# A kernel with a planned instruction order: shorter least time per scan unit in the plan, 1/std spread for two chunks at once, step sizes written to SBUF by VectorE

## The chip, the cores and the metric

The kernel runs on one core of one Trainium2 chip. The metric is the device time of one execution in microseconds (us). Before the change it is 8340.93 us, the median of three runs (8316.7 to 8378.94).

Five engines matter: TensorE (PE in the profile, its weight loads PEld), VectorE (DVE), ScalarE (ACT), GpSimd (POOL) and SyncE (SP, which here only issues DMAs). Each takes its own instructions strictly in program order and waits on semaphores for the others. SBUF is the working memory, PSUM (8 banks of 128x512 float32) is where TensorE writes.

## The reference

Four layers work on four images x of 96 channels and 64x64 pixels (L = 4096 positions). Cut to what matters:

```python
x = x + L0(_gn(x))        # layer norm, in-projection, 3x3 depthwise conv, silu,
                          # selective scan in 4 directions, layer norm, gate, out-projection
x = x + L1(_gn(x))        # deformable 3x3 conv: offsets and mask from a conv, 4 bilinear corners
t = t + L2_attn(_ln_t(t)) # FFT over the 4096 tokens, diagonal complex product, inverse FFT
t = t + L2_ffn(_ln_t(t))  # 96 -> 384 -> 96, fp8-like rounding
t = t + L3_attn(_ln_t(t)) # attention without softmax
t = t + L3_ffn(_ln_t(t))

# the selective scan, per image, direction k (4), channel d (192), state n (16):
delta = softplus(dts + delta_bias)            # the "step size"
h = exp(delta * A) * h + (delta * u) * B      # along 4096 positions
y = sum_n h * C
```

## The kernel before, in words

**Stages.** Layer 0 has a preparation per image (group norm, layer norm, convolution, `projected`, and `steps`, which makes the step sizes delta and delta*u) and the scan itself. `Layer0.behind` normalizes, gates and projects the scan's sum; `Layer1` computes offsets and then samples (`sample`: 1152 indirect gathers on GpSimd); `Fourier`, `Ffn`, `LinearAttention` and `Ffn` follow. Everything passes between the stages through DRAM, except for the last image.

**The scan is the metronome.** It is cut into 1536 units (4 images x 4 directions x 4 pieces of 1024 positions x 24 groups of 8 channels), one after the other. A unit has: a broadcast load of delta (L999, issued by ACT, 512 KB), exp on ACT (L1027), two bf16 matmuls that spread delta*u into a PSUM tile `db` (L1033), a product with B on VectorE (`enter`, L1047), the scan instruction on VectorE (`recur`, L1055), a product with C on GpSimd (`weigh`, L1064) and matmuls that sum over the state (`total`, L1078 and L1083).

**Everything else is woven in by a planner.** Two generator streams run beside the scan: `ends` (preparation of images 0 to 3, then layers 2 and 3 of every image) and `middle` (`behind` and layer 1 of every image). While the program is built, `Clock` keeps an estimated end for each engine. After each unit, `unit()` moves the plan's time `due` forward by `PACE` (L203, 4.5), and the plan's "now" is the later of `due` and the planned end of VectorE's queue (L224). Streams then add steps as long as each engine that a step uses is planned to be done no later than now plus a margin (`AHEAD`, L197). The costs given at each `yield cost(...)` are the planner's own. They set only the order: after building, every engine's instructions are tied to that order (`in_program_order`). When the last unit is placed, what is left of the streams follows by itself, with the scan's PSUM banks given to `ends` (`own_banks`: 5 banks for `ends`, 3 for `middle`; until then both share 3). I call this part the tail.

**PSUM banks in the plan.** A chain of steps may begin a step that needs a fresh bank only if `has_bank` allows (L289); `holds` says how many banks it keeps.

**Spread of 1/std.** Both layer norms (`normed_rows` L732 to L743, `normed` L1732 to L1745) keep 1/std of 8 chunks of 512 positions as rows of one 128x512 tile. `spread` (L527 to L532) brings one row to all partitions by a float32 matmul over all 128 rows with a column of the identity as weights (L531); VectorE then multiplies the chunk by it from PSUM (L738, L1742). One chain per chunk, three chains side by side.

**Step sizes.** `steps` (L827 to L900) runs 192 times, for one direction's 128 channels or two directions' 64. VectorE forms max(pd,0)+lw in place in PSUM (L856), multiplies it by u, still from PSUM, into `ex` (L861, L862, L868 or L874), and ACT copies it from PSUM to the SBUF tile `rl` (L877). SP stores `rl` to DRAM (L881). The bank is held until the copy is issued.

Of the kernel before, what the change touches and what calls it, by code (L numbers as in the profile page):

```python
# [14 lines left out]
AF = mybir.ActivationFunctionType  # L15
ALU = mybir.AluOpType
# [3 lines left out]
B, C, H, W = 4, 96, 64, 64  # L20
# [5 lines left out]
CH = 512  # L26
NCH = L // CH
# [155 lines left out]
def cost(pe=0.0, dve=0.0, act=0.0, pool=0.0, **more):  # L183
    return Step((pe, dve, act, pool), **more)


def wait(us=0.0, **more):

    return Step((0.0,) * 4, us, **more)
# [10 lines left out]

MARGIN = 0.5

PACE = 4.5  # L203


class Clock:
# [19 lines left out]
    def unit(self, scanned):  # L226

        self.due += PACE
        self.idle, self.beside = max(scanned, self.due), 0.0
# [42 lines left out]
def pipe(net, chains, width, every=0, lane=None, **tiles):  # L272


    chains, active = iter(chains), []
    clock, known, more = net.clock, net.known, True
    end, free = clock.now(), tiles
    while True:
        if more and len(active) < width:
            steps = next(chains, None)  # L280
            if steps is None:
                more = False
            else:
                active.append(Chain(steps, clock.now()))
                continue
        if not active:
            break
        for n, chain in enumerate(active):
            if chain.new and not net.has_bank(1 + (n > 0 and not active[0].holds)):  # L289
                continue  # L290
            if any(
                a.done <= chain.done + every
                for a in active[:n]
                if lane is None or (a.kind is lane) == (chain.kind is lane)
            ):
                continue
            if not all(free.get(tag, net.arrived.get(tag, 0)) > 0 for tag in chain.takes):
                continue
            if clock.has_room(known.get((chain.kind, chain.done), (1.0,) * 4), chain.ready):
                break  # L300
        else:
            yield BLOCKED
            continue
        for tag in chain.takes:
            if tag in free:
                free[tag] -= 1
        clock.precede(known.get((chain.kind, chain.done), (0.0,) * 4))
        step = next(chain.steps, None)
        if step is None:
            net.hold(-chain.holds)  # L310
            active.remove(chain)
            end = max(end, chain.ready)
            continue
        for tag in step.frees:
            free[tag] += 1
        known[chain.kind, chain.done] = step.work
        chain.ready = clock.queue(step, chain.ready)
        chain.done += 1
        net.hold(step.holds - chain.holds)
        chain.holds, chain.new, chain.takes = step.holds, step.new, step.takes  # L320
        yield None
    yield wait(max(0.0, end - clock.now()))
# [38 lines left out]
class Net:  # L361
# [165 lines left out]
    def spread(self, rstd, j, n, key):  # L527

        pb = self.mm(f"lnb{key}_{j}")
        row = self.ident[:, j : j + 1].to_broadcast([128, 128])  # L530
        self.nc.tensor.matmul(pb, lhsT=row, rhs=rstd, start=True, stop=True)  # L531
        return pb[:n]  # L532


# [24 lines left out]
class Layer0:  # L559
# [117 lines left out]
    @staticmethod  # L677
    def rows(pad, j):
        return pad[:, 1 + j * NR : 1 + (j + 1) * NR, 1 : 1 + W]

    @staticmethod
    def as_rows(t):
        return t.rearrange("p (h w) -> p h w", w=W)
# [25 lines left out]
    def normed_rows(self, b, x, pad):  # L709

        net, rows, as_rows = self.net, self.rows, self.as_rows
        tc, nc = net.tc, net.nc
        with tc.tile_pool(name=f"l0n{b}", bufs=2) as sm:
            for edge in (pad[:, 0, :], pad[:, PW - 1, :], pad[:, :, 0], pad[:, :, PW - 1]):
                nc.gpsimd.memset(edge, 0.0)
            yield wait(4.0)
            stats = []
            yield from net.group_norm_stats(x, sm, f"0_{b}", stats)
            mean, rstd = stats

            cen = sm.tile([C, 128], F32, name=f"cen{b}", tag="cen", bufs=1)
            nc.vector.tensor_scalar_mul(cen, net.cen96, rstd)
            yield cost(dve=0.3)
            net.hold(1)
            pb = net.mm(f"cb{b}")
            nc.tensor.matmul(pb[:, 0:1], lhsT=cen, rhs=mean, start=True, stop=True)
            bias = sm.tile([C, 1], F32, name=f"cenb{b}", tag="cenb", bufs=1)
            nc.scalar.mul(bias, pb[:C, 0:1], -1.0)
            net.hold(-1)
            yield cost(pe=0.3, act=0.3)  # L730

            rs = yield from net.centred(x, cen, lambda j: (rows(pad, j), as_rows), f"0_{b}", sm, bias)  # L732

            def chain(j):
                pb = net.spread(rs, 32 * (j % 4) + j // 4, C, f"0_{b}")
                yield cost(pe=1.2, holds=1)
                r = rows(pad, j)
                nc.vector.tensor_mul(r, r, as_rows(pb))  # L738
                yield cost(dve=0.7)
                nc.scalar.activation(r, r, AF.Identity, scale=net.vec(V_ING, C), bias=net.vec(V_INB, C))  # L740
                yield cost(act=0.8)

            yield from pipe(self.net, (chain(j) for j in range(NCH)), 3)  # L743

    def conv_weights(self, b, sm):

# [80 lines left out]
    def steps(self, b, ks, j, us, dtw, sm, xdbl):  # L827

        net = self.net
        nc = net.nc  # L830
        cs = slice(j * CH, (j + 1) * CH)
        tk = f"{b}_{j}_" + "".join(str(k) for k in ks)
        both = len(ks) == 2

        def tile_of(name, bufs):
            return sm.tile([128, CH], F32, name=f"{name}{tk}", tag=name, bufs=bufs)
# [4 lines left out]
        pd = net.mm(f"pd{tk}")  # L841
# [3 lines left out]
        ex = tile_of("ex", 3)  # L845
        nc.scalar.activation(ex, pd, AF.Abs)
        nc.scalar.activation(ex, ex, AF.Exp, scale=-1.0)
        lw, w1 = tile_of("lw", 2), tile_of("w1", 2)
        nc.scalar.activation(lw, ex, AF.Ln, bias=net.one)
        nc.scalar.activation(w1, ex, AF.Identity, bias=net.one)  # L850
        yield cost(pe=2.2 if both else 1.1, act=2.7, holds=1, takes="rl")
        nc.vector.scalar_tensor_tensor(w1, w1, -1.0, ex, ALU.add, ALU.subtract)  # L852
        yield cost(dve=0.7, holds=1)
        nc.gpsimd.tensor_sub(lw, lw, w1)  # L854
        yield cost(pool=1.3, holds=1)
        nc.vector.scalar_tensor_tensor(pd, pd, 0.0, lw, ALU.max, ALU.add)  # L856
        if both and ks[0] % 2 == ks[1] % 2:
            q, xc = ks[0] % 2, us[2]
            own, far = slice(64 * q, 64 * q + 64), slice(64 - 64 * q, 128 - 64 * q)
            turned = xc.rearrange("p (a b) -> p b a", a=64)  # L860
            nc.vector.tensor_mul(ex[own], pd[own], xc[own, cs])  # L861
            nc.vector.tensor_mul(  # L862
                ex[far].rearrange("p (a b) -> p a b", b=64),
                pd[far].rearrange("p (a b) -> p a b", b=64),
                turned[far, j * NR : (j + 1) * NR, :],
            )
        elif not both and ks[0] % 2:
            nc.vector.tensor_mul(  # L868
                ex.rearrange("p (w h) -> p w h", h=H),
                pd.rearrange("p (w h) -> p w h", h=H),  # L870
                us[1][:, j * NR : (j + 1) * NR, :],
            )
        else:
            nc.vector.tensor_mul(ex, pd, us[2 if both else 0][:, cs])  # L874
        yield cost(dve=1.4, holds=1, frees="lw")
        rl = tile_of("rl", 2)
        nc.scalar.copy(rl, pd)  # L877
        yield cost(act=0.6)
        parts = ((0, 64, ks[0], 128), (64, 128, ks[1], 128)) if both else ((0, 128, ks[0], 0),)
        for p0, p1, k, c0 in parts:  # L880
            nc.sync.dma_start(self.de_d[b][k][c0 : c0 + p1 - p0, cs], rl[p0:p1])  # L881
        yield wait(takes="du", frees="rl")

        du = sm.tile([128, 3, CH], BF16, name=f"du{tk}", tag="du", bufs=2)
        nc.scalar.copy(du[:, 0, :], ex)
# [7 lines left out]
            pr, lhsT=self.minus, rhs=du[:, 1, :], start=False, stop=True, skip_group_check=True  # L893
# [838 lines left out]
def normed(net, t, tl, key, pool, groups=(0, 1), arriving=False):  # L1732

    rs = yield from net.centred(
        t, net.cen96, lambda j: (tl[:C, j * CH : (j + 1) * CH], plain), key, pool, groups=groups, arriving=arriving
    )

    def chain(j):
        cs = slice(j * CH, (j + 1) * CH)
        pb = net.spread(rs, 32 * (j % 4) + groups.index(j // 4), C, key)  # L1740
        yield cost(pe=1.2, holds=1)
        net.nc.vector.tensor_mul(tl[:C, cs], tl[:C, cs], pb)  # L1742
        yield cost(dve=0.7)

    yield from pipe(net, (chain(j) for j in chunks(groups)), 3)  # L1745


def chunks(groups):
    return [4 * r + q for r in groups for q in range(4)]
# [324 lines left out]
```

## Time and profile before

| | us |
|---|---|
| median of three runs (lowest, highest) | 8340.93 (8316.7, 8378.94) |
| the profiled execution's own time | 8389.31 |
| its span, first to last instruction | 8387.5 |
| scan units, first scan to last scan's end | 191.6 to 7376.2 |
| tail after the last scan | 7376.2 to 8387.5 |
| sampling of the last image, all in the tail | 7497.7 to 7986.8 |
| layers 2 and 3 of image 2, end | 7910.5 |

The profile gives for every engine the busy time, for every group of equal instructions the count, mean duration and the idle time ahead of it with the releaser (what ended that wait), and for a stretch of time the busy time of each engine and the granted TensorE clock (1.0 is full speed). The mean granted clock of the execution is 0.790. A busy TensorE is not TensorE at its peak, since matmuls are pipelined and their ends modelled.

### The profile page before, as it was taken

To read this page: it belongs to the slowest core of one execution; us is meant where nothing else is said; L and a number is where in the kernel's file an instruction comes from. 1 tells how busy PE (TensorE), PEld (TensorE's weight loads), DVE (VectorE), ACT (ScalarE), POOL (GpSimd) and SP (SyncE) were. 2 spreads that over 40 slices of the span, in tenths; PEclk is the share of its full clock that TensorE was granted. 3 is DMA by queue.
4 is the path that set the end of the run, shared out by engine and by line. 5 is a ranking of instruction groups with operands and counts; after the bars stand their busy time and mean duration, and the time that the engine had idled before them with its cause. 6 is when DMAs were issued, how large, how long until landed. Compare 5 with 4: busy or idle time off the path is not lost.

```text
span 8387.5 us, 96574 instructions
## 1 busy us (share of the span) xinstructions
PE 6457.2 (77%) x32232; PEld 2791.3 (33%) x32232; DVE 6737.2 (80%) x5149; ACT 5007.3 (60%) x9177; POOL 5539.7 (66%) x4268
## 2 busy tenths in 40 slices
PE   6776777779767778877767888776888787887787
PEld 2211221122222233311222555221455332455473
DVE  2799889987799988777898888998887988846724
ACT  5665567646577877855667666644467766333324
POOL 0466556665578888656688888766688897626700
PEclk8876786778667878966677898786788887887798
DMA  3577678886778998876789899877799888844420
GB/s 91 160 213 201 170 191 223 224 196 185 190 213 242 248 250 220 216 184 176 216 221 243 220 233 235 189 174 181 192 229 243 209 217 207 181 107 130 133 67 13
DMA packets 791030, 1600.42 MB, mean 191 GB/s; under 512 B 285889, under 2 KB 374493, under 8 KB 788422
## 3 DMA queue, kind: packets, MB, share of 16 engines
q10 hardware_dynamic: 244224, 843.17, 39.3%
q1 hardware_dynamic: 472582, 524.50, 24.0%
q0 software_dynamic: 73728, 226.57, 10.2%
q8 instruction: 259, 4.24, 0.2%
q14 instruction: 237, 1.94, 0.1%
HBM read 1340.71 MB, written 253.14 MB: 190 GB/s over the span
## 4 chain that ended last, share of the span: by engine, by line
PE 31%; DVE 27%; DMA 11%; POOL 11%; ACT 9%; issue 8%; SPq 2%; ACTq 1%; DVEq 0%; another core or an unknown queue 0%; POOLq 0%
DVE da L1055 13%; POOL da L1064 7%; DVE db L1047 6%; PE pc L767 4%; PE f L1635 3%; PE py L1083 3%; PE ps L1528 3%; ACT g L1507 2%; POOL g L1495 2%; DMA da<-de 2%; ACT da L1027 2%; PE db L1033 2%; PE pd L1547 2%; DMA du<-du 2%; DMA m<-in_dft 1%
## 5 line engine op out<-in xcount | busy, mean ns | idle before, releaser
L1064 POOL TENSOR_TENSOR da<-da,bc 128x1024 f32<-128x1024 f32 x1536 | 3634.9, 2369 | 317.2 <-DVE da L1055 191.5
L1055 DVE TENSOR_TENSOR_SCAN da<-da,st,db 128x1024 f32<-128x1024 f32 x1152 | 2700.9, 2345 | 116.1 <-ACT da L1027 7.7
L1047 DVE TENSOR_TENSOR db<-db,bc 128x1024 f32<-128x1024 f32 x1536 | 1865.6, 1215 | 659.9 <-PE db L1033 644.2
L1027 ACT ACTIVATE da<-da,w_al 128x1024 f32<-128x1024 f32 x1536 | 1740.5, 1146 | 313.6 <-DMA da<-de 123.4
L1495 POOL DMA_INDIRECT g<-table,idx x1152 | 1191.1, 1034 | 408.1 <-issue 183.1
L1033 PE MATMUL db<-du,rep 24*128 24x512 bf16 x3072 | 687.4, 455 | 797.3 <-DVE da L1055 741.5
L1083 PE MATMUL py<-da,w_fold 128*32 128x512 f32 x6144 | 1103.2, 787 | 26.5 <-POOL da L1064 11.0
L1507 ACT ACTIVATE g<-g,wt 128x96 f32<-128x96 f32 x3456 | 966.0, 364 | 115.2 <-issue 19.0
L1055 DVE TENSOR_TENSOR_SCAN da<-da,db 128x1024 f32<-128x1024 f32 x384 | 877.2, 2284 | 66.1 <-ACT da L1027 31.7
L1528 PE MATMUL ps<-w_ident,g 128*96 128x128 f32 x3744 | 689.4, 331 | 224.5 <-ACT g L1507 67.3
L1033 PEld LDWEIGHTS <-rep 24*128 24x128 bf16 x3072 | 147.3, 93 | 1867.8 <-DVE da L1055 1128.9
L1528 PEld LDWEIGHTS ps<-w_ident,g 128*96 128x96 f32 x3744 | 500.0, 148 | 560.4 <-ACT g L1507 171.3
L1062 POOL COPY st<-da 128x1 f32<-128x1 f32 x1152 | 224.8, 195 | 697.7 <-DVE da L1055 664.4
L854 POOL TENSOR_TENSOR lw<-lw,w 128x512 f32<-128x512 f32 x192 | 244.3, 1272 | 660.7 <-DVE w L852 595.9
L767 PE MATMUL pc<-pad,wc 96*128 96x512 f32 x1152 | 570.6, 633 | 13.3 <-ACT xa L777 6.1
L1536 ACT COPY st<-ps 96x384 f32<-96x384 f32 x384 | 179.7, 472 | 483.1 <-PE ps L1528 418.8
L888 PE MATMUL pr<-ex,w_ident 128*128 128x512 f32 x384 | 297.3, 866 | 60.2 <-ACT st L1536 15.1
L767 PEld LDWEIGHTS pc<-pad,wc 96*128 96x128 f32 x1152 | 218.4, 200 | 313.9 <-issue 285.4
L844 PE MATMUL pd<-xd,w_dtw 103*64 103x512 f32 (+1 forms) x512 | 273.3, 798 | 57.3 <-ACT rl L877 15.2
L1547 PE MATMUL pd<-st,wdc 96*128 96x256 f32 x1152 | 303.8, 411 | 7.1 <-ACT st L1536 3.4
L1644 ACT COPY d<-f 128x512 f32<-128x512 f32 x192 | 111.6, 582 | 328.0 <-PE f L1635 274.1
L890 ACT CAST du<-pr 128x512 bf16<-128x512 f32 x192 | 111.7, 582 | 321.4 <-PE pr L889 259.7
(286 smaller groups left out, 8861.6 us busy)
## 6 DMA issues: line engine op xcount, KB each, us to landing
da<-de ACTq DMA_DIRECT2D x1536, 512.0 KB
du<-du SPq DMA_DIRECT2D x1536, 96.0 KB
bc<-bcd SPq DMA_DIRECT2D x128, 512.0 KB
y<-yb SPq DMA_DIRECT2D x384, 128.0 KB
de<-rl SPq DMA_DIRECT2D x128, 256.0 KB
m<-in_dft SPq DMA_DIRECT2D x128, 256.0 KB
ad<-y ACTq DMA_DIRECT2D x192, 128.0 KB
table<-pix SPq DMA_DIRECT2D x128, 192.0 KB
```

Source lines behind the costliest of these rows:

```text
L767: nc.tensor.matmul(pp, lhsT=wc[:, q, g * 128 : (g + 1) * 128], rhs=pad[:, r0 + dy : r0 + dy + NR, dx : dx + W], start=(q == 0), stop=(q == 8),
L888: nc.tensor.matmul(pr, lhsT=net.ident, rhs=ex, start=True, stop=False)
L1027: self.net.nc.scalar.activation(u.da, u.da, AF.Exp, scale=self.al[:, a : a + 1])
L1033: self.net.nc.tensor.matmul(db[:, h, :], lhsT=self.rep[64 * u.q + 32 * h : 64 * u.q + 32 * h + 24], rhs=u.du[64 * u.q + 32 * h : 64 * u.q ...
L1047: self.net.nc.vector.tensor_mul(u.db, u.db, u.bc[:, 0, :])
L1055: nc.vector.tensor_tensor_scan(u.along(u.hh), u.along(u.da), u.along(u.db), first, ALU.mult, ALU.add)
L1064: self.net.nc.gpsimd.tensor_mul(u.hh, u.hh, u.bc[:, 1, :])
L1083: nc.tensor.matmul(py[p0 : p0 + 32], lhsT=self.fold[:, u.i, :], rhs=hc[:, h * CH : (h + 1) * CH], start=u.sums["add"] is None and u.i == 0 ...
L1495: nc.gpsimd.indirect_dma_start(out=g[:, k, :], out_offset=None, in_=self.tables[b % 2], in_offset=bass.IndirectOffsetOnAxis(ap=idx[:, n : ...
L1507: nc.scalar.activation(pixel, pixel, AF.Identity, scale=wt[:, n, c : c + 1])
L1528: nc.tensor.matmul(pt[:, k, :], lhsT=g[:, k, c * C : (c + 1) * C], rhs=net.ident, is_transpose=True, start=(c == 0), stop=(c == corners - 1),)
L1547: nc.tensor.matmul(po, lhsT=wdc[:, k, :], rhs=st[k // 3][:, k % 3, :], start=(k == 0), stop=(k == 8))
```

## The change

Three edits. `PACE` goes from 4.5 to 4.3. The layer norms take two chunks per chain: both spreads are issued one after the other, each over only the 32 rows that hold its value, into two PSUM banks; a chain starts only when two banks are free, and two chains run side by side. In `steps`, VectorE writes the step size to the SBUF tile `rl` instead of PSUM, the product with u reads `rl`, ACT's copy is gone, and the planned hold of the bank ends with that write.

```diff
-PACE = 4.5
+PACE = 4.3
...
-            if chain.new and not net.has_bank(1 + (n > 0 and not active[0].holds)):
+            if chain.new and not net.has_bank(chain.new + (n > 0 and not active[0].holds)):
...
     def spread(self, rstd, j, n, key):
         pb = self.mm(f"lnb{key}_{j}")
-        row = self.ident[:, j : j + 1].to_broadcast([128, 128])
-        self.nc.tensor.matmul(pb, lhsT=row, rhs=rstd, start=True, stop=True)
+        k = slice(j - j % 32, j - j % 32 + 32)
+        row = self.ident[k, j : j + 1].to_broadcast([32, 128])
+        self.nc.tensor.matmul(pb, lhsT=row, rhs=rstd[k], start=True, stop=True)
         return pb[:n]
...
-    def chain(j):
-        cs = slice(j * CH, (j + 1) * CH)
-        pb = net.spread(rs, 32 * (j % 4) + groups.index(j // 4), C, key)
-        yield cost(pe=1.2, holds=1)
-        net.nc.vector.tensor_mul(tl[:C, cs], tl[:C, cs], pb)
-        yield cost(dve=0.7)
-
-    yield from pipe(net, (chain(j) for j in chunks(groups)), 3)
+    def chain(js):
+        yield wait(new=2)
+        pbs = [net.spread(rs, 32 * (j % 4) + groups.index(j // 4), C, key) for j in js]
+        yield cost(pe=1.2, holds=2)
+        for n, j in enumerate(js):
+            cs = slice(j * CH, (j + 1) * CH)
+            net.nc.vector.tensor_mul(tl[:C, cs], tl[:C, cs], pbs[n])
+            yield cost(dve=0.7, holds=1 - n)
+
+    js = chunks(groups)
+    yield from pipe(net, (chain(js[n : n + 2]) for n in range(0, len(js), 2)), 2)
```

`normed_rows` is changed in the same way. In `steps`:

```diff
         yield cost(pe=2.2 if both else 1.1, act=2.7, holds=1, takes="rl")
+        rl = tile_of("rl", 2)
...
-        nc.vector.scalar_tensor_tensor(pd, pd, 0.0, lw, ALU.max, ALU.add)
+        nc.vector.scalar_tensor_tensor(rl, pd, 0.0, lw, ALU.max, ALU.add)
+        yield cost(dve=0.7, frees="lw")
...
-            nc.vector.tensor_mul(ex, pd, us[2 if both else 0][:, cs])
-        yield cost(dve=1.4, holds=1, frees="lw")
-        rl = tile_of("rl", 2)
-        nc.scalar.copy(rl, pd)
-        yield cost(act=0.6)
+            nc.vector.tensor_mul(ex, rl, us[2 if both else 0][:, cs])
         parts = ((0, 64, ks[0], 128), (64, 128, ks[1], 128)) if both else ((0, 128, ks[0], 0),)
         for p0, p1, k, c0 in parts:
             nc.sync.dma_start(self.de_d[b][k][c0 : c0 + p1 - p0, cs], rl[p0:p1])
-        yield wait(takes="du", frees="rl")
+        yield cost(dve=0.7, takes="du", frees="rl")
```

The other two forms of the product (L861 and L862, L868) read `rl` in the same way.

More of the change, by code (lines that the diff above doesn't have):

```diff
@@ L734, in chain @@
             def chain(j):
-                pb = net.spread(rs, 32 * (j % 4) + j // 4, C, f"0_{b}")
-                yield cost(pe=1.2, holds=1)
-                r = rows(pad, j)
-                nc.vector.tensor_mul(r, r, as_rows(pb))
-                yield cost(dve=0.7)
-                nc.scalar.activation(r, r, AF.Identity, scale=net.vec(V_ING, C), bias=net.vec(V_INB, C))
-                yield cost(act=0.8)
-            yield from pipe(self.net, (chain(j) for j in range(NCH)), 3)
+                yield wait(new=2)
+                pbs = [net.spread(rs, 32 * ((j + i) % 4) + (j + i) // 4, C, f"0_{b}") for i in range(2)]
+                yield cost(pe=1.2, holds=2)
+                for i in range(2):
+                    r = rows(pad, j + i)
+                    nc.vector.tensor_mul(r, r, as_rows(pbs[i]))
+                    yield cost(dve=0.7, holds=1 - i)
+                    nc.scalar.activation(r, r, AF.Identity, scale=net.vec(V_ING, C), bias=net.vec(V_INB, C))
+                    yield cost(act=0.8, holds=1 - i)
+            yield from pipe(self.net, (chain(j) for j in range(0, NCH, 2)), 2)
     def conv_weights(self, b, sm):
@@ L860, in steps @@
             turned = xc.rearrange("p (a b) -> p b a", a=64)
-            nc.vector.tensor_mul(ex[own], pd[own], xc[own, cs])
+            nc.vector.tensor_mul(ex[own], rl[own], xc[own, cs])
             nc.vector.tensor_mul(
                 ex[far].rearrange("p (a b) -> p a b", b=64),
-                pd[far].rearrange("p (a b) -> p a b", b=64),
+                rl[far].rearrange("p (a b) -> p a b", b=64),
                 turned[far, j * NR : (j + 1) * NR, :],
@@ L869, in steps @@
                 ex.rearrange("p (w h) -> p w h", h=H),
-                pd.rearrange("p (w h) -> p w h", h=H),
+                rl.rearrange("p (w h) -> p w h", h=H),
                 us[1][:, j * NR : (j + 1) * NR, :],
@@ L1736, in normed @@
     )
-    def chain(j):
-        cs = slice(j * CH, (j + 1) * CH)
-        pb = net.spread(rs, 32 * (j % 4) + groups.index(j // 4), C, key)
-        yield cost(pe=1.2, holds=1)
-        net.nc.vector.tensor_mul(tl[:C, cs], tl[:C, cs], pb)
-        yield cost(dve=0.7)
-    yield from pipe(net, (chain(j) for j in chunks(groups)), 3)
+    def chain(js):
+        yield wait(new=2)
+        pbs = [net.spread(rs, 32 * (j % 4) + groups.index(j // 4), C, key) for j in js]
+        yield cost(pe=1.2, holds=2)
+        for n, j in enumerate(js):
[4 more added lines that the diff above has]
+    yield from pipe(net, (chain(js[n : n + 2]) for n in range(0, len(js), 2)), 2)
 def chunks(groups):
```

## The prediction, made before the changed kernel ran

> **What bounds the kernel now.** I read the page first: its span, the busy line and the groups.
>
> ```profile
> span 8387.5 us, 96574 instructions
> PE 6457.2 (77%) x32232; PEld 2791.3 (33%) x32232; DVE 6737.2 (80%) x5149; ACT 5007.3 (60%) x9177; POOL 5539.7 (66%) x4268
> ...
> L1055 DVE TENSOR_TENSOR_SCAN da<-da,st,db 128x1024 f32<-128x1024 f32 x1152 | 2700.9, 2345 | 116.1 <-ACT da L1027 7.7
> L1047 DVE TENSOR_TENSOR db<-db,bc 128x1024 f32<-128x1024 f32 x1536 | 1865.6, 1215 | 659.9 <-PE db L1033 644.2
> ```
>
> No engine is full. VectorE is nearest, and each of the 1536 units costs it 1.21 + 2.33 = 3.54 us; its largest idle time, 644.2 us, is the product `db` waiting for TensorE's two matmuls (L1033), which stand in TensorE's queue behind other streams' work. Then I cut time into the sixteen stretches of 96 units and the tail, by the view of windows (length, then PE, PEld, DVE, ACT and POOL busy, granted clock, DMA). Five stretches and the tail's three parts:
>
> ```profile
> 2479.10:2893.60 414.50, 300.92 (x1336) 117.92 (x1336) 379.89 (x258) 324.05 (x718) 364.90 (x289) 0.80 0.90 243
> 3320.30:3817.60 497.30, 399.94 (x1415) 137.81 (x1414) 373.09 (x249) 331.49 (x558) 325.56 (x245) 0.82 0.79 198
> 3817.60:4304.30 486.70, 339.89 (x1294) 105.13 (x1292) 418.57 (x314) 290.89 (x497) 321.20 (x244) 0.69 0.75 203
> 4738.30:5170.80 432.50, 375.16 (x3122) 250.08 (x3120) 355.47 (x228) 293.93 (x715) 365.89 (x294) 0.89 0.93 236
> 6508.30:6922.90 414.60, 322.83 (x1543) 140.90 (x1543) 368.60 (x241) 303.99 (x703) 369.00 (x295) 0.82 0.83 212
> 7376.20:7911.00 534.80, 421.28 (x2772) 275.81 (x2771) 330.31 (x496) 167.85 (x326) 288.32 (x252) 0.82 0.42 123
> 7911.00:7987.00 76.00, 45.58 (x140) 25.12 (x140) 53.76 (x68) 17.64 (x36) 52.64 (x45) 0.70 0.45 136
> 7987.00:8387.50 400.50, 339.99 (x2991) 245.36 (x2990) 132.41 (x226) 129.18 (x243) 7.45 (x2) 0.89 0.11 36
> ```
>
> A unit takes 414.5/96 = 4.32 us in the lightest stretch and 5.18 in the heaviest, 4.68 on average (7184.6/1536). The plan's least time of 4.5 is therefore not what a unit takes: it decides how much other work is put beside it. In the tail TensorE carries the time: 421 of 535 us while layers 2 and 3 of image 2 run beside the last image's sampling, 340 of 400 us when only the last image's layers 2 and 3 are left. The time is thus 191.6 (start) + 7184.6 (scan) + 1011.3 (tail).
>
> **The change part by part**
>
> *Least time 4.3: what moves.* The changed program can be set beside the old one in order of instructions. Its other work slips: the first gather of image 1's sampling comes at unit 873 (was 825), of image 2's at 1274 (was 1220), and after the last unit there now stand image 1's attention and second FFN, all of image 2's layer 2 (most of its first FFT half was done before), all four pairs of the last image's `behind` and two of image 2's 32 sampled tiles. Counting instructions and pricing each at its line's busy time in the trace over its count, the work that is not the scan's own is, inside the scan and in the tail:
> PE 3821 and 880 us before, 3518 and 1172 after; DVE 897 and 562 before, 827 and 665 after; ACT 3051 and 328, then 2756 and 460; POOL 1390 and 313, then 1310 and 373. So 292 us of TensorE work leave the scan for the tail.
>
> *Scan, lighter units.* Over the sixteen stretches a least-squares line is: time of a unit = 2.52 + 0.59 x PE + 1.16 x DVE us, both the other work per unit (rms 0.15; ACT and POOL add nothing, 0.01 and -0.05). With the new order's contents it gives 261 us less; over 64 stretches of 24 units the slopes are 0.37 and 1.00 and give 184 less. The line goes too low where little is left: one stretch would take 3.76 us with 3.74 us of VectorE work in it. Holding each stretch at VectorE's work plus 0.25 us (the idle of the quietest short stretches) leaves -201; comparing stretch with stretch by hand, each with one of like content, gives only -110. I take -185, near the finer fit, ends -261 and -110.
>
> *Step size in SBUF.* `rl` from PSUM costs the write what it cost (0.69 us, L856). The product of u with `rl` instead of PSUM has two SBUF inputs. VectorE's nearest such instruction at that place is L852:
>
> ```profile
> L852 DVE SCALAR_TENSOR_TENSOR w<-w,ex x192: 665/682/3885, 111.5 to 4559.4; 128x512 f32<-128x512 f32 x192
> ```
>
> ```profile
> L856 DVE SCALAR_TENSOR_TENSOR pd<-pd,lw x192: 667/687/705, 113.5 to 4578.9; 128x512 f32<-128x512 f32 x192
> L877 ACT COPY rl<-pd x192: 558/585/605, 117.3 to 4580.3; 128x512 f32<-128x512 f32 x192
> L874 DVE TENSOR_TENSOR ex<-pd,xa x64: 691/691/693, 114.3 to 4579.6; 128x512 f32<-128x512 f32 x64
> L868 DVE TENSOR_TENSOR ex<-pd,xa x64: 1016/1036/1096, 525.7 to 4517.2; 128x512 f32<-128x512 f32 x64
> ```
>
> (minimum, median, maximum in ns.) With an operand in PSUM the spread is 705 - 667 ns; with both in SBUF it reaches 3885. The timeline shows why:
>
> ```profile
> 4210.77 4.66 POOL L1064 TENSOR_TENSOR da<-da,bc 128x1024 f32<-128x1024 f32 x2
> 4210.88 0.69 DVE L856 SCALAR_TENSOR_TENSOR pd<-pd,lw 128x512 f32<-128x512 f32 x1
> 4211.60 1.03 DVE L868 TENSOR_TENSOR ex<-pd,xa 128x512 f32<-128x512 f32 x1
> 4212.55 3.44 DVE L852 SCALAR_TENSOR_TENSOR w<-w,ex 128x512 f32<-128x512 f32 x1
> ```
>
> L852 ends only as GpSimd's product ends (4215.43), and L868, its operand in PSUM, ran through it. The Trainium skill, "SBUF — State Buffer", section "SBUF: two separate sides", has the rule: a VectorE instruction with two SBUF inputs and a GpSimd instruction that reads SBUF exclude each other for a whole instruction. This trace agrees, and the rule speaks against this edit; by it alone every product that starts during a GpSimd product waits that one out. The price goes by rows. Low end: L852's mean over its median, 864 - 682 = 182 ns, times 192: 35 us. High end: laying today's products over GpSimd's products, 111 of 208 begin inside one, with 166 us left in all. The products themselves are the nearest row, but after a stall the engines stand otherwise, so 120. These stalls are VectorE time in the scan, at a slope of about 1.
>
> Gains of the same edit: ACT loses 192 x 0.58 = 112 us, worth nothing while its slope is 0.01; the bank comes free and the store can start before the product. SP's queue waited 409.1 us in all for the copy at L881, and behind it stand the units' loads, but TensorE waited only 39.8 us for those (`du`); its rows that name the copy as releaser have 12 to 24 us each. So -15, ends 0 and -60. Added waits: VectorE may now wait for the store of two `rl` earlier; ACT waited 2.9 us for it, once. Behind it on VectorE would stand the next `db` product, and the scan and GpSimd behind that; 0 to 3 us.
>
> *Spreads in pairs.* 192 spreads of 1.27 us busy each (243.1 us for L531). No run has a 32-row float32 pair; the nearest row is L1033, two bf16 matmuls over 24 rows of different quarters, whose starts lie 4 ns apart. So a pair takes between one spread's time and two: 0 to 122 us of TensorE less, nearly three fifths of it ahead of the tail. The Trainium skill, "TensorE: Matmul & The Clock Gate", section "Why this matters for your kernels", says that matmuls with few rows run side by side in distinct row groups; L1033 agrees, and by that alone the 122 would come whole. At a slope of 0.4 to 0.6 the scan gains 30 (0 to 45); the tail's share is taken below.
>
> *Tail.* 292 us at mean prices are 268 at the tail's (its rows show 807 busy where mean prices give 880), less 38 for pairs there (80 spreads; three quarters of what full overlap gives): 230. At full density that is +230; at the joint part's density (421/535) +290; without any gain from pairs 268/0.79 = +340. By chain: image 2's FFN, attention, FFN took 259 us (7652 to 7911), one FFT half 224 beside the sampling and 105 alone; `ends` now has two halves, image 1's attention and FFN (166) and these before the last image can start. The last gather stands ahead of image 2's second FFN there, so sampling no longer ends last. I take +260, ends +215 and +340. What hides nothing here: no scan is left to cover it.
>
> Sum: -185 + 120 - 15 - 30 + 260 = +150. The profiled execution takes 8389.3 (span 8387.5), 0.6% over the runs' median of 8340.9; the change is applied to the median: **8490 us**, 1.8% slower. About 1% (83 us) is what a measurement of this kernel can tell from no change.
>
> **The rivals**
>
> *The scan follows the least time* (faster): each unit shrinks by the whole 0.2 us, -307, and stalls cost only 35. For it: three of the four 24-unit stretches with under 1.7 us of other PE take 3.9 to 4.2 us. Against: nine of the sixteen would hold over 0.5 us of other VectorE work, a floor above 4.04 before any wait. -307 + 35 - 45 + 240 = -77: 8264 us. It decides from the point where the scan as a whole loses more than 260 us, 0.17 a unit.
>
> *The tail hides it*: TensorE idles 113.5 + 30.4 = 144 us in the joint part; if the longer streams fill that, only 230 - 144 = +86 remain: 86 - 110 = -24, 8317 us, no difference. Against: `ends` is a chain, and idle time inside a chain stays.
>
> *Stalls and tail both at their upper ends*: -110 + 166 + 340 = +396, 8737 us. For it: a stalled VectorE delays the scan, and GpSimd's queue waits on the scan.
>
> *The pairs don't help*: two banks at once are rarely free, chains wait: inside the range (+30 to +68).
>
> **How the numbers follow.** Forecast (+60 to +280, 8400 to 8620): 0.56; scan follows: 0.18; tail hides: 0.14; upper ends (over +280): 0.12. Half of "scan follows" lies beyond -83, and 0.02 of "tail hides": faster 0.11. The rest of both and 0.06 of the forecast: same 0.27. Slower 0.62. The range leaves out half of "scan follows" and most of the upper ends: 8300 to 8640.
>
> **What would show it.** The last scan should end some 110 us earlier, so near 7265 on this profile's scale, and the tail be near 1270. The products into `ex` should spread from 0.69 to over 2.5 us, their mean 0.5 above the median; L1033's idle total should fall; paired L531 should start a few ns apart. Wrong: a scan shorter by over 260, a tail under 1150, or products without a spread.

## The result, and the profile after

| | before | after |
|---|---|---|
| median of four runs each (lowest, highest), us | 8329.58 (8316.7, 8378.94) | 8545.83 (8543.57, 8559.55) |
| ratio of the times, 95% interval | | 1.0252 [1.0207, 1.0297] |
| profiled execution's span, us | 8387.5 | 8541.8 |

The changed kernel is slower by 2.5%; the forecast was 1.8%. The two spans differ by 154 us where the sum said 150, the medians by 216: the profiled execution of before lay 0.7% above its own median, that of after at its median. So a term read off the two traces can be some 60 us off, and that the spans differ by nearly what the sum said is partly due to the execution of before that was traced. Small terms need the experiments below.

The page of the changed kernel, with the lines that answer to those of before (span, busy time, the two groups that make a unit):

```profile
span 8541.8 us, 96681 instructions
PE 6473.0 (76%) x32196; PEld 2770.2 (32%) x32196; DVE 6846.1 (80%) x5209; ACT 4891.5 (57%) x8905; POOL 5584.0 (65%) x4252
...
L1056 DVE TENSOR_TENSOR_SCAN da<-da,st,db 128x1024 f32<-128x1024 f32 x1152 | 2700.6, 2344 | 121.9 <-ACT da L1028 12.3
L1048 DVE TENSOR_TENSOR db<-db,bc 128x1024 f32<-128x1024 f32 x1536 | 1862.4, 1213 | 583.7 <-PE db L1034 581.2
```

ACT is busy 4891.5 us instead of 5007.3, nearly the 111 us that its 192 copies took. VectorE is busy 109 us longer; the products with u, below, account for 102. The wait of `db` for TensorE fell from 644.2 to 581.2 us, and a unit's two instructions cost what they did.

Time is then cut at the last scan's end. The columns are length, busy time of PE, PEld, DVE, ACT and POOL, granted clock, DMA share and GB/s. Before, the scan:

```profile
191.60:7376.20 7184.60, 5526.29 (x26069) 2197.26 (x26069) 6186.97 (x4300) 4595.79 (x8445) 5182.26 (x3956) 0.78 0.81 208
```

After, the scan and the tail's three parts (to the end of sampling, to the end of image 2's layers, to the end):

```profile
193.60:7291.40 7097.80, 5320.39 (x24485) 2044.79 (x24484) 6195.60 (x4197) 4364.71 (x7936) 5148.77 (x3892) 0.76 0.81 207
7291.40:8076.00 784.60, 646.87 (x4323) 419.31 (x4320) 448.44 (x647) 265.59 (x533) 415.28 (x343) 0.83 0.48 122
8076.00:8136.00 60.00, 43.78 (x122) 17.11 (x122) 34.17 (x72) 26.95 (x52) 0.00 (x0) 0.75 0.00 0
8136.00:8541.80 405.80, 333.13 (x2999) 238.41 (x2997) 134.62 (x233) 138.07 (x259) 10.87 (x3) 0.87 0.13 40
```

The scan became 87 us shorter (7185 to 7098) and ended at 7291, where 7265 had been forecast. The tail became 239 us longer (1011 to 1250; forecast 1270). Nearly all of it lies ahead of the last image's layers: that last part is 400 us before and 406 after. In the whole tail TensorE is busy 1024 us, 217 more than before: the moved work is paid for at 1.1 us for each us of TensorE.

The products with u, and ahead of them the step size that they read (minimum, median and maximum in ns, then first and last start):

```profile
L860 DVE SCALAR_TENSOR_TENSOR rl<-pd,lw x192: 658/679/692, 114.3 to 4755.5; 128x512 f32<-128x512 f32 x192
L879 DVE TENSOR_TENSOR ex<-rl,xa x64: 676/693/2824, 115.0 to 4757.3; 128x512 f32<-128x512 f32 x64
L873 DVE TENSOR_TENSOR ex<-rl,xa x64: 1015/1058/2898, 537.9 to 4677.0; 128x512 f32<-128x512 f32 x64
L879 DVE TENSOR_TENSOR ex<-rl,xc x48: 678/692/5077, 1235.7 to 4704.4; 128x512 f32<-128x512 f32 x48
```

The write, one operand in PSUM, still spreads over 34 ns only. The products, both operands in SBUF, have the old median and a maximum of 2.8 to 5.1 us; 65 of 208 take over 1.3 us, and what all of them take above their medians is 102 us. The timeline around the longest one:

```profile
4703.70 0.68 DVE L860 SCALAR_TENSOR_TENSOR rl<-pd,lw 128x512 f32<-128x512 f32 x1
4704.29 4.64 POOL L1065 TENSOR_TENSOR da<-da,bc 128x1024 f32<-128x1024 f32 x2
4704.42 5.08 DVE L879 TENSOR_TENSOR ex<-rl,xc 128x512 f32<-128x512 f32 x1
...
4710.02 2.33 DVE L1056 TENSOR_TENSOR_SCAN da<-da,st,db 128x1024 f32<-128x1024 f32 x1
```

The product starts 0.13 us after the first of two GpSimd products and ends only after both (4708.93). It is the one case of this kind: the other 64 long ones outlast a single GpSimd instruction. Behind it, the next scan stands in VectorE's queue.

### The profile page after: what moved, and what is told of

Its sections match the earlier page's. It is cut to its first block, busy times and chain, and to the rows that moved or that the text cites. A ratio compares the mean times of both kernels' runs of the same rounds, so it can differ in the third digit from the quotient of the medians.

```text
span 8541.8 us, 96681 instructions
## 1 busy us (share of the span) xinstructions
PE 6473.0 (76%) x32196; PEld 2770.2 (32%) x32196; DVE 6846.1 (80%) x5209; ACT 4891.5 (57%) x8905; POOL 5584.0 (65%) x4252
## 5 line engine op out<-in xcount | busy, mean ns | idle before, releaser
L1048 DVE TENSOR_TENSOR db<-db,bc 128x1024 f32<-128x1024 f32 x1536 | 1862.4, 1213 | 583.7 <-PE db L1034 581.2
L1496 POOL DMA_INDIRECT g<-table,idx x1152 | 1211.2, 1051 | 346.1 <-issue 168.6
L770 PE MATMUL pc<-pad,wc 96*128 96x512 f32 x1152 | 588.1, 646 | 7.8 <-DVE rl L860 4.2
L1084 PEld LDWEIGHTS py<-da,w_fold 128*32 128x32 f32 x6144 | 160.0, 125 | 399.4 <-issue 303.7
```

Of the source, the lines that this page charges most:

```text
L770: nc.tensor.matmul(pp, lhsT=wc[:, q, g * 128 : (g + 1) * 128], rhs=pad[:, r0 + dy : r0 + dy + NR, dx : dx + W], start=(q == 0), stop=(q == 8),
L1048: self.net.nc.vector.tensor_mul(u.db, u.db, u.bc[:, 0, :])
L1084: nc.tensor.matmul(py[p0 : p0 + 32], lhsT=self.fold[:, u.i, :], rhs=hc[:, h * CH : (h + 1) * CH], start=u.sums["add"] is None and u.i == 0 ...
L1496: nc.gpsimd.indirect_dma_start(out=g[:, k, :], out_offset=None, in_=self.tables[b % 2], in_offset=bass.IndirectOffsetOnAxis(ap=idx[:, n : ...
```

## The experiments

Four theories on where the 2.5% come from are named in the expectations. **P**: the shorter least time, by the work that it moves into the tail, with the waits for GpSimd on top. **S**: the step-size edit, above all its waits. **B**: the chains that need two banks at once. **N**, which came up only after e2: the order itself. The old order happens to be a good one, and whatever changes the plan, if only by a little, loses by it. Twelve kernels were run; ratios are to the kernel before on the same chip, with 95% intervals. All readings off their traces stand in one table, in us: scan (first scan to last scan's end), the tail up to the last engine's end, TensorE's busy time in each, VectorE's idle time ahead of all 1536 `db`, what the products take above their medians, the time in which any spread runs, and the granted clock of the traced execution. The tails are 5 to 6 us shorter here than by the span.

| kernel | ratio | scan | tail | PE scan / tail | idle before `db` | products | spreads | clock |
|---|---|---|---|---|---|---|---|---|
| before | 1 | 7185 | 1005 | 5526 / 807 | 660 | 1 | 243 | .790 |
| after | 1.0252 | 7098 | 1245 | 5320 / 1024 | 584 | 102 | 178 | .773 |
| e1 least time 4.3 alone | 1.0249 | 6966 | 1418 | 5239 / 1162 | 535 | 0 | 242 | .780 |
| e2 after, 4.5 | 1.0268 | 7409 | 983 | 5625 / 763 | 726 | 98 | 191 | .768 |
| e3 after, bank held | 1.0400 | 7164 | 1384 | 5417 / 1091 | 626 | 114 | 190 | .754 |
| e3, product from PSUM | 1.0325 | 7072 | 1371 | 5326 / 1070 | 657 | 0 | 189 | .768 |
| e4 after, 128 rows | 1.0216 | 7078 | 1241 | 5299 / 1026 | 577 | 105 | 231 | .789 |
| e5 step size alone | 1.0213 | 7387 | 970 | 5592 / 786 | 693 | 100 | 248 | .785 |
| e6 spreads alone | 1.0116 | 7261 | 954 | 5561 / 754 | 729 | 0 | 179 | .778 |
| e7 before, 4.52 | 1.0130 | 7265 | 965 | 5553 / 766 | 686 | 0 | 238 | .795 |
| e8 before, 4.40 | 1.0173 | 7108 | 1181 | 5340 / 981 | 640 | 0 | 245 | .789 |
| e9 before, 4.55 | 1.0191 | 7315 | 963 | 5584 / 760 | 683 | 0 | 245 | .791 |
| e10 before, 4.60 | 1.0171 | 7295 | 976 | 5554 / 761 | 690 | 0 | 247 | .793 |
| e11 spreads, 4.60 | 1.0171 | 7322 | 945 | 5624 / 698 | 702 | 1 | 184 | .779 |

### e1: the shorter least time alone

```diff
-PACE = 4.5
+PACE = 4.3
```

The kernel before, and nothing else changed.

> The kernel before with only the least time per unit at 4.3. Theory P (the shorter least time takes work out of the scan, where it was half hidden, into the tail, where it is not): in its order 369 us of TensorE work (by mean prices) leave the scan for the tail, against 292 in the changed kernel, whose tail grew by 239; so the tail grows by some 300 to about 1310 us, the scan gets 150 to 250 shorter, and the whole is 50 to 150 us slower than before. Rival S (the products' waits for GpSimd are the loss, the least time by itself is neutral or a gain): within 40 us of before or faster, the scan shorter by as much as the tail grows. Rival B (chains that need two banks are the loss): as rival S here.

Measured: 8588.48 us, 1.0249 [1.0220, 1.0278]. The windows of its scan and its tail:

```profile
191.28:7157.55 6966.27, 5238.64 (x24126) 2028.36 (x24129) 6107.28 (x4171) 4375.50 (x7920) 5064.57 (x3855) 0.77 0.83 210
7157.55:8581.21 1423.66, 1162.43 (x7738) 745.05 (x7730) 683.38 (x1050) 463.87 (x922) 433.23 (x367) 0.84 0.32 84
```

The scan loses 218 us, the tail gains 413. Alone, the edit moves more TensorE work past the last scan than it does in the changed kernel (356 us more busy time against 217), and pays 413/356 = 1.16 us for each. So this edit by itself makes a loss of the whole size. That is what P says, though the loss, 199 us between the medians, is above the 50 to 150 expected.

### e2: the changed kernel with the old least time

```diff
-PACE = 4.3
+PACE = 4.5
```

> The changed kernel with the least time back at 4.5. Its tail has 860 us of TensorE work where before has 880. Theory P: the tail is near 960 to 1010 us, the scan is longer than before's by the products' waits (102 us in the changed kernel) less what pairs give (65 us of TensorE at most, half of it felt): in all 0 to 70 us slower than before, so most of the 216 us are gone. Rival S: 100 us or more slower than before. Rival B: also 100 or more slower, with TensorE or the banks as what VectorE waits for.

Measured: 8598.34 us, 1.0268 [1.0238, 1.0298]. With the tail's cost gone (983 us, below before's 1005) the kernel is as slow as ever: its scan takes 7409 us, 224 more than before's, and VectorE is idle for 726 us ahead of `db`, 695 of them waiting for TensorE. P as the only cause has fallen. From e2 to the changed kernel the shorter least time takes 311 us off the scan and puts 262 on the tail; the ratio hardly moves.

### e3: the product from SBUF and from PSUM, in one order

To take away the waits for GpSimd and nothing else, two kernels were built that differ only in what the product reads. Both keep the bank until after the product, so that the plan is the same:

```diff
-        yield cost(dve=0.7, frees="lw")
+        yield cost(dve=0.7, holds=1, frees="lw")
```

In the second, the product also reads PSUM (all four forms). It leaves the softplus out of the product with u, which then takes the projection as it stands; its time is that of a product with an operand in PSUM.

```diff
-            nc.vector.tensor_mul(ex, rl, us[2 if both else 0][:, cs])
+            nc.vector.tensor_mul(ex, pd, us[2 if both else 0][:, cs])
```

> The changed kernel with the bank of the step size held in the plan until the product with u is placed; the product still reads SBUF. It is the control for the next run and has its order. Close to the changed kernel, 8500 to 8590 us, with 90 to 120 us of waits in the products (sum over their medians).

> The same order as the control, but the product with u reads the PSUM tile again (which holds the step size before softplus, so the softplus is left out of the product and the output differs). Only the operand's place is changed. Theory S-size: if the waits are VectorE time on the path, the products stay at 0.69 and 1.04 us without a tail, and the time falls by the 100 us of waits, at least by 60. Rival (the waits are absorbed, since VectorE waits for TensorE's matmuls afterwards anyway): products as short, but the time falls by less than 40 us.

Measured: 8735.46 us, 1.0400 [1.0361, 1.0440], and 8653.11 us, 1.0325 [1.0302, 1.0348]. The products of the second:

```profile
L873 DVE TENSOR_TENSOR ex<-pd,xa x64: 993/1026/1101, 528.1 to 4741.1; 128x512 f32<-128x512 f32 x64
```

```profile
L879 DVE TENSOR_TENSOR ex<-pd,xa x64: 670/681/685, 115.0 to 4826.5; 128x512 f32<-128x512 f32 x64
```

No product takes over 1.1 us. 114 us of waits are gone, the scan is 92 us shorter (7164 to 7072), the median 82 us: most of each us of these waits is felt. That is 0.7 to 1% of the kernel's time, by the ratios and by the scan, and comes from the SBUF operand alone. The first of the two was expected near the changed kernel, at 8500 to 8590 us, and missed that by far: the longer hold alone took the kernel from 1.0252 to 1.0400. So a new plan cost something here too.

### e4: the pairs over 128 rows

The order of the changed kernel, instruction for instruction; only the spreads go over all 128 rows again, and so cannot run side by side.

```diff
-        k = slice(j - j % 32, j - j % 32 + 32)
-        row = self.ident[k, j : j + 1].to_broadcast([32, 128])
-        self.nc.tensor.matmul(pb, lhsT=row, rhs=rstd[k], start=True, stop=True)
+        row = self.ident[:, j : j + 1].to_broadcast([128, 128])
+        self.nc.tensor.matmul(pb, lhsT=row, rhs=rstd, start=True, stop=True)
```

> The changed kernel in its very order, but each spread again over all 128 rows, so that two of a pair can't run side by side. Only the matmuls' rows differ. Theory P: TensorE's time in these matmuls rises from 178 to some 243 us, about 30 us of it in the tail where it is felt whole and 35 in the scan where less than half is: 30 to 60 us slower than the changed kernel, a ratio to before of 1.029 to 1.032. Rival (the pairs hide in TensorE's own waits): within 15 us of the changed kernel.

Measured: 8519.0 us, 1.0216 [1.0169, 1.0263]. P's range, 1.029 to 1.032, is missed; the rival's 15 us lie within the noise. The changed kernel's own 1.0252 [1.0207, 1.0297] is no better; by the ends of the two intervals, pairs that would save the 68 us (0.8%) of the forecast are hardly possible. Yet they do run side by side. Spreads in the second FFN of the last image, TensorE's timeline of the changed kernel:

```profile
8400.61 4.19 PE L532 MATMUL lnbf<-lnsf,w_ident 32*128 32x512 f32 x14 [3.30 <-DVE lnsf L439]
8405.92 2.07 PE L532 MATMUL lnbf<-lnsf,w_ident 32*128 32x512 f32 x2 [1.11 <-DVE fl L1745]
```

and of e4, at the same place of the program:

```profile
8371.68 8.83 PE L532 MATMUL lnbf<-lnsf,w_ident 128*128 128x512 f32 x16 [3.31 <-DVE lnsf L439]
```

Each spread leaves two records, one after the other, so these are eight spreads each: 6.3 us of TensorE against 8.8. In the changed kernel the first records of four spreads, two pairs, start within 20 ns, and their second records 1.0 us later; in e4 each record starts after the one ahead, by 0.43 us where the clock is full. Where both kernels have a granted clock of 1.00 the gain is large. Four spreads of the layer norm that follows, the changed kernel first:

```profile
8454.36 1.14 PE L532 MATMUL lnb<-lns,w_ident 32*128 32x512 f32 x8
```

```profile
8433.22 3.62 PE L532 MATMUL lnb<-lns,w_ident 128*128 128x512 f32 x8
```

Where did the gain go? The lines of this matmul show it (minimum, median, maximum in ns), first the changed kernel's, then e4's:

```profile
L532 PE MATMUL lnb<-lns,w_ident x192: 585/1056/1218, 54.7 to 8463.9; 32*128 32x512 f32 x192
```

```profile
L532 PE MATMUL lnb<-lns,w_ident x192: 591/593/1223, 55.1 to 8436.2; 128*128 128x512 f32 x192
```

Both can take 0.59 us and both can take 1.22; the usual one is near the short end with 128 rows and near the long end with 32. The windows of three such places have the reason in the column ahead of the last two, the granted clock. The changed kernel, then e4:

```profile
945.10:965.20 20.10, 15.17 (x40) 3.62 (x40) 19.86 (x16) 8.28 (x10) 10.15 (x8) 0.50 0.37 96
...
7435.10:7452.50 17.40, 17.39 (x28) 4.75 (x28) 10.58 (x17) 2.93 (x4) 10.87 (x8) 0.50 0.31 55
...
8400.60:8408.00 7.40, 6.26 (x16) 1.75 (x17) 6.06 (x10) 0.00 (x0) 0.00 (x0) 0.50 0.00 0
```

```profile
933.90:953.90 20.00, 14.44 (x40) 4.08 (x40) 19.76 (x16) 8.10 (x10) 10.16 (x8) 0.84 0.42 99
...
7405.70:7420.50 14.80, 14.76 (x28) 5.45 (x28) 11.51 (x18) 2.93 (x4) 10.86 (x8) 0.88 0.40 70
...
8371.70:8380.50 8.80, 8.80 (x16) 3.62 (x17) 6.44 (x10) 0.00 (x0) 0.00 (x0) 0.81 0.00 0
```

Around 32-row spreads the clock is at half, around the same spreads over 128 rows at 0.81 to 0.88. In the second pair of lines the same 28 matmuls take 17.4 us with pairs and 14.8 without. Over all spreads and the 8 us after each, the mean granted clock is 0.62 in the changed kernel (617 us of such time) and 0.85 in e4 (632 us); everywhere else it is 0.78 in both. TensorE's work other than spreads is busy 6314 us against 6227 in e4: 87 us more, against 53 us less in the spreads. The Trainium skill, "TensorE: Matmul & The Clock Gate", section "What's actually happening", says that a monitor sets the clock to full or half by how busy TensorE has lately been; the half is what these rows show, but in the second window TensorE is busy all the time in both kernels (17.39 of 17.40 us and 14.76 of 14.80), and the clock is at half in one of them. So its busy time in the trace alone doesn't tell the clock here. The two kernels differ both in the rows of a spread and in how many run at once; which of the two brings the clock down was not tried.

### e5 and e6: each of the other two edits alone

e5 is the kernel before with the edit in `steps` alone, e6 with the two-chunk chains and `has_bank` alone; both at 4.5. Their diffs are the parts of the change shown above.

> The kernel before with only the step-size edit, least time 4.5, spreads as before. The changed kernel at 4.5 took 2.7% longer than before with a scan 224 us longer, of which 98 us are the products' waits; the rest is open. Theory S (the step-size edit makes all of it: waits, plus the plan that frees the bank early and packs other matmuls ahead of the next unit's): scan 150 to 230 us longer, ratio 1.018 to 1.027. Theory B (the pairs' two banks at once make the rest): scan about 80 to 110 us longer, ratio 1.009 to 1.014. Theory N (the rest is the order's own scatter: any other plan costs as much): not foretold by the edit.

> The kernel before with only the paired spreads, least time 4.5. Theory S: no stalls in the products, scan within 30 us of before's, tail 20 us shorter: ratio 0.994 to 1.003. Theory B: scan 100 us or more longer with VectorE's waits for TensorE grown by as much: ratio 1.01 to 1.015.

Measured: e5 8525.83 us, 1.0213 [1.0165, 1.0260]; e6 8431.61 us, 1.0116 [1.0065, 1.0167]. In e5 the products wait 100 us, and the scan takes 202 us longer; the waits are half of that. It lies in the range of theory S. e6 has no such waits, and its scan still takes 76 us longer; its ratio lies in the range of theory B, which was to be the rival of S. Of the three edits each alone costs 1 to 2.5%, and all three together 2.5%: they don't add up, and no one edit is the cause.

### e7 to e10: a new plan and nothing else

If any new order costs, a change without meaning must cost too. The least time of the kernel before is set to 4.52 (e7), 4.40 (e8), 4.55 (e9) and 4.60 (e10); no operation differs.

```diff
-PACE = 4.5
+PACE = 4.52
```

> The kernel before with the least time at 4.52 instead of 4.50: a change that means nothing by itself but gives another order throughout. Theory N: the time moves by 40 us or more, up or down, with as much in the scan's waits for TensorE. Otherwise it stays within 25 us (ratio 0.997 to 1.003).

> The kernel before with the least time at 4.40, one of three points that give the curve between 4.3 (2.5% slower) and 4.52 (1.3% slower). Its order moves 230 us of TensorE work from the scan to the tail. Theory P (a shorter least time loses by itself): tail some 190 us longer, scan 100 to 150 shorter, a ratio of 1.013 to 1.02, beyond the scatter only if it is clearly above the points on the other side. Theory N (any new order costs about 1.2%, the least time nothing): 1.008 to 1.016, no slope.

> The kernel before with the least time at 4.55. TensorE work goes the other way: 42 us less in the tail. Theory P: scan longer, tail 35 shorter, a ratio of 1.00 to 1.005 by contents. Theory N: 1.008 to 1.016, as at 4.52.

> The kernel before with the least time at 4.60: 59 us less TensorE work in the tail. By contents the scan gains 45 to 70 us and the tail loses 50: 1.000 to 1.003. Theory N: 1.008 to 1.016.

Measured: e7 8436.47 us, 1.0130 [1.0080, 1.0180]; e8 8479.35, 1.0173 [1.0127, 1.0220]; e9 8491.02, 1.0191 [1.0157, 1.0224]; e10 8470.09, 1.0171 [1.0135, 1.0208]. A least time longer by 0.4% costs 1.3%, and none of the four neighbours, above or below, has a ratio under 1.013 (e7's interval reaches down to 1.008). At 4.40 P foretold as much, so the three above 4.50 speak for N; e9 and e10 lose more than the 1.008 to 1.016 that it expected. So in the orders tried, 1.3 to 1.9% went with the old order. A rival is that 4.50 is the best point of a smooth curve. Against it, 0.02 us more for each of 1536 units is 31 us, while e7's scan is 80 us longer, and 4.60 loses no more than 4.55. How 4.50 was chosen is not known; if it was kept as the fastest of many values, neighbours that lose are no surprise.

In e7 the loss is in the scan, 80 us longer while the tail is 40 shorter. (The two traces differ by 38 us, the medians by 87.) The fourth sixteenth of its scan against before's, by the windows, e7 first:

```profile
1543.00:2047.20 504.20, 392.00 (x1137) 106.42 (x1136) 394.81 (x282) 276.39 (x351) 285.50 (x207) 0.75 0.77 184
```

```profile
1538.50:1996.40 457.90, 357.00 (x1112) 98.21 (x1112) 396.22 (x290) 265.50 (x347) 289.95 (x212) 0.78 0.83 201
```

VectorE does the same 395 us of work in 504 and in 458 us, and `db` waits 75.8 us for TensorE there instead of 33.5: TensorE is busy 35 us longer there, with 1137 matmuls instead of 1112, and they stand at other places among the units. Over the whole program VectorE's idle time ahead of `db` grew by only 26 us (660 to 686), so this stretch shows one way to lose and not the sum. The clock differs as well: over all runs on the same chips its mean is 0.799 to 0.800 for the kernel before and 0.787 to 0.794 for e7 to e10. (The 0.790 of before in the table is of the traced execution; the runs of before beside the experiments had 0.793 to 0.804.) Whether the new orders bring the clock down, and how much of the loss goes with it, was not separated. What makes the order at 4.50 the better one is not in any single line, and stays open.

### e11: the spreads with another least time

e6 with a least time of 4.60.

> Paired spreads alone, least time 4.60: no product waits, tail with 800 us of TensorE work, the least of all orders tried. If any of these orders beats before it is this one: 0.995 to 1.005 if the order costs nothing by itself, 1.008 to 1.015 by theory N.

Measured: 8470.59 us, 1.0171 [1.0136, 1.0207]. e10, at 4.60 without the pairs, has 1.0171 too: between two orders neither of which is the old one, no gain from the pairs shows. This is weaker than e4, since the two orders differ, and orders alone scatter from 1.013 to 1.019 in e7 to e10. Both ratios lie above theory N's range. Here again the clock is lower with them, 0.779 against 0.793 in the profiled executions.

No kernel that was run is faster than the one before.

## Why the prediction was right, and where its steps were not

**Sign and size** held: 1.0252 where 1.018 was forecast, +216 us between the medians (+154 between the spans) where the sum said +150, inside its +60 to +280. The bounds that would have shown it wrong were not reached: a scan shorter by over 260 (87), a tail under 1150 (1250), products without a spread.

**Lighter units, -185 (ends -261 and -110).** e1 measures the term by itself: -218, with 356 us of TensorE work moved instead of 292. From e2 to the changed kernel it is -311, beyond the end at -261. So the size held from before's order and depends on the order. The same is true of the point that the scan would not follow the least time (0.2 us a unit would be -307): from e2 it does.

**Step size in SBUF, +120 (ends 35 and 166).** 102 us in the changed kernel; in one order (e3) 114 us in the trace, 92 in the scan. Held. The rule that the prediction drew from the Trainium skill, "SBUF — State Buffer", "SBUF: two separate sides", agrees with e3, where the waits are 114 us with two operands in SBUF and 0 with one in PSUM; it gives no price, and the price came from laying the products over GpSimd's.

**Copy and bank, -15.** The copies are gone from ACT. The wait ahead of `db` fell, as forecast, but it fell further in e1, where the copy stayed, so it tells nothing of this term. Not settled.

**Pairs, -30 in the scan and -38 in the tail.** This is the step that failed. The matmuls do run side by side, but at a mean clock of 0.62 around them, and the work around them slows by more (87 us) than the spreads gain (53); e4 shows no gain in time. The prediction took the duration of a record as fixed by its kind and asked only how far two would overlap. Its rival "the pairs don't help" named the right size for another reason: it held that free banks would be lacking.

**Tail, +260 (ends +215 and +340).** +239, at 1.1 us for each us of moved TensorE work. Held, though without the 38 us for pairs, so the rest of that term, 298, was some 60 us too high; e1, whose plan moved more than the changed kernel's, shows that the price and not the amount was the general part: 413 us, above the upper end.

**The rivals.** *The scan follows* needed -260 in the scan; there were -87. *The tail hides it* needed the moved work in TensorE's gaps; TensorE's idle time in the tail grew from 204 to 227 us. *Both at their upper ends* needed over +280; there were +216 between the medians.

**What the prediction did not see.** It added the edits up on the ground of before's order, as if that order were an average one. By its terms the two edits other than the least time would cost 120 - 15 - 30 - 38 = +37 us; e2 has them alone and loses 2.7%, its scan +224 us. So the total came out right in part by luck. The tail's cost and the waits were real and of the size forecast, but the gain of the pairs was not there and the loss of the old order was not counted. The losses also don't add up: e1 and e2 lose as much as the changed kernel, one in its tail, the other in its scan. How much of the changed kernel's 2.5% belongs to the old order stays open.

## What to carry to other kernels

Where a planner sets the order, run the old kernel with a meaningless change of the plan first: here 4.52 instead of 4.50 cost 1.3%, and an edit that loses less than that has shown nothing about itself. Leave one operand of a VectorE product in PSUM while GpSimd works from SBUF (0.7 to 1% of this kernel), and don't count a matmul over fewer rows as saved time before its granted clock has been looked at. Work that is moved past the stage that covers it costs its full time there: 1.0 to 1.2 us for each us here (from e2 to the changed kernel 262 us for 261, in e1 413 for 356).

## What the runs showed of the hardware

- The granted clock fell to 0.50 around 32-row float32 matmuls where it was 0.81 to 0.88 around the same matmuls over 128 rows, with TensorE busy all the time in one such window of each kernel. Every run of a kernel with 32-row spreads had a mean clock of 0.754 to 0.782; those with 128-row spreads had 0.780 to 0.804.
- Four 32-row spreads in different quarters of the rows run at once: 1.14 us in all where the clock is 1.00, against 3.62 us for four over 128 rows. At a clock of 0.50 their records take 1.06 to 1.22 us each instead of 0.59 to 0.69.
- One VectorE product with both operands in SBUF lasted through two GpSimd products in a row, 5.08 us for 0.69 us of work, so GpSimd's second seems to have gone ahead of the waiting VectorE. The other 64 long ones outlast one GpSimd instruction each.
